# The statistics of the last layer: most of their combining moved into the recurrence's last block, on GpSimd

## The chip, the cores and the metric

One core of a Trainium2 chip (trn2) runs one program. The metric is device microseconds for one execution, as the median of several runs. The engines are TensorE (PE in the profile; its weight loads are PEld), VectorE (DVE), ScalarE (ACT), GpSimd (POOL) and SyncE (SP), which here only issues transfers. The engines run side by side, each its own list of instructions in order, and wait for each other through semaphores.

## What is computed

The reference takes x of shape (8, 32, 256, 256), in fp32, through four layers. Each adds its result to its input, and each normalises its input first (group norm, 16 groups of two channels):

```python
x = x + L0(gn(x))   # Fourier layer: 32 x 32 low modes, mixed over channels
x = x + L1(gn(x))   # one 5 x 5 convolution for every channel
x = x + L2(gn(x))   # recurrence over the 256 columns: a gated cell, 3 rows wide
x = x + L3(gn(x))   # running maxima in four directions, mixed over channels
def _gn(v, G=16, eps=1e-5):
    g = v.reshape(B_, G, C_ // G, H_, W_)
    m = jnp.mean(g, axis=(2, 3, 4), keepdims=True)
    s = jnp.var(g, axis=(2, 3, 4), keepdims=True)
    return ((g - m) / jnp.sqrt(s + eps)).reshape(v.shape)
```

The change concerns the mean and the variance that the last of these normalisations needs: one pair for each image and each pair of channels, over all of the output of the third layer.

## The kernel before

The kernel has three stages, one after the other: the Fourier layer with the convolution (to about 952 us), the recurrence with the running maxima towards the right (to about 2314 us), and the other maxima with the last mixing.

**Recurrence** (`recurrence`, L787). The 256 columns are cut into 32 blocks of 8 (`NB`, `WB`). A column is done in two half steps, x = 0 and x = 1, with four images each; below, half steps are counted n = 2 * column + x within a block, so those with x = 0 are even and those with x = 1 odd. In a half step (`step`, L916) TensorE forms the gates' sums, ScalarE their sigmoids (L937, L939, L940) and the tanh (L944), VectorE the four elementwise steps L938, L943, L951 and L953, whose result is the new state hs. GpSimd does two: the product L946 (one gate times the normalised column xn), for which L951 is made to wait, and the sum L954, which adds the new state to the layer's input and so makes the layer's output in place, in the block's tile xw. Between L946 and L954 the program can put one more instruction for GpSimd: in block 0 it is a normalisation (L838), in half steps 2 to 5 and 8 to 11. All other normalisations are ScalarE's (L842).

Finished blocks leave work for the steps that follow, one piece in each half step, in front of L951: in even ones the running maximum fm of a column (L975), in odd ones the statistics of one image of the block before (L986, a bn_stats instruction that gives counts, means and sums of squared deviations for two halves of its 512 elements). So the statistics of block 30 are made during block 31, and those of block 31, eight instructions, after the last step. SP stores the blocks to memory (L964): x3d, the layer's output, and fwd, the running maxima.

**Combining.** The tile bst holds for every partition, image and block two triples (count, mean, sum of squared deviations); `parts` shows it as 64 triples for each image, so means lie three elements apart. L1020 to L1024 square all the means, add the sums of squared deviations over the count, sum both over the 64 halves, and divide by 64. The matrix `pair` (1/8 where two channels are of one group) then adds up partitions of a group in one matmul (L1075).

**Maxima** (`maxima_and_mix`, L1027) go through the blocks from the last to the first. Blocks 30 and 31 come first: x3_30, x3_31 and fw_30 are loaded through ScalarE's queue (L1117, L1123) in that order, behind all that ScalarE has to do for the recurrence, fw_31 through SP's. The order of VectorE's work is written out by hand: the first maximum of block 30 (L1153), the four short steps of the variance (L1078 to L1081) with a power on GpSimd (L1082) behind them, further maxima (L1156, L1163), the scaled weights (L1087 to L1094), and so on; L1146 is the first instruction that reads x3_31, and L1148 makes the running maximum towards the left, rv.

**Memory.** Pools of tiles are laid one above the other. The recurrence's small pool (`bc`: states, bst, second) lies under its pools for xn, xw, fm and the working tiles. The third stage lays its own pools over the same memory, so its first loads wait for the last readers of the tiles beneath.

Of the kernel before, what the change touches and what calls it, by code (L numbers as in the profile page):

```python
# [9 lines left out]
F32 = mybir.dt.float32  # L10
AF = mybir.ActivationFunctionType
ALU = mybir.AluOpType
AX = mybir.AxisListType
# [3 lines left out]
P = 128  # L17
B, C, H, W = 8, 32, 256, 256
# [6 lines left out]
Q = H // A  # L25
# [761 lines left out]
def recurrence(tc, k, d, x2d, x3d, fwd, stb, first, loaded, mean1, mv3):  # L787
# [4 lines left out]
    nc = tc.nc  # L792
    WB = 8
    NB = W // WB
    NH = 4
    NC = 2
    BC = B // NC
    with ExitStack() as ctx:
        one = ctx.enter_context(tc.tile_pool(name="bc", bufs=1, reuse_waits="tile"))
# [19 lines left out]
        for t in hs[0] + hs[1]:  # L819
            nc.vector.memset(t[:, :, 0 : Q + 2 : Q + 1], 0.0)  # L820
        bst = one.tile([P, B, NB, 6], F32, name="bst")

        raws, norms, psums = {}, {}, {}

# [29 lines left out]
        def free(ins):  # L854

            if some[0]:
                tc.declare_no_dep(ins.ins, group="signals", reason="later matmuls of the same half step end last")
# [28 lines left out]
        def own(n, gate):  # L886

            w, x = divmod(n, NC)
            if w >= W:
                return  # L890
            key = ("r", "z", "nh")[gate]
            out = psums[n, key] = ps.tile([P, BC, Q], F32, name=f"{key}_{n}", tag=f"{key}{x}")
            within(out, OWN, gate, norms[w // WB][:, x * BC : (x + 1) * BC, w % WB, :], True, gate == N)
# [22 lines left out]
        def step(w, x, extra=None):  # L916
            bi, wi = w // WB, w % WB
            bs = slice(x * BC, (x + 1) * BC)
            raw, cur = raws[bi][:, bs, wi, :], norms[bi][:, bs, wi, :]
            new = hs[x][w % NH][:, :, 1 : 1 + Q]  # L920
            if w == 0:
                nc.vector.tensor_copy(new, cur)
            else:
                n, prev = NC * w + x, hs[x][(w - 1) % NH]
                if n == NC:
                    for gate in (Z, R, N):
                        own(n, gate)
                    nc.tensor.drain().then_inc(sem, 1)
                    count[0] += 1
                gates(n, prev)  # L930
                p = {g: psums.pop((n, g)) for g in ("r", "z", "ni", "nh")}
                r = wk.tile([P, BC, Q], F32, name=f"rs_{w}_{x}", tag=f"rs{x}")
                m = wk.tile([P, BC, Q], F32, name=f"n_{w}_{x}", tag=f"n{x}")
                zm = wk.tile([P, BC, Q], F32, name=f"zm_{w}_{x}", tag=f"zm{x}")
                a = wk.tile([P, BC, Q], F32, name=f"a_{w}_{x}", tag=f"a{x}")
                z = wk.tile([P, BC, Q], F32, name=f"zs_{w}_{x}", tag=f"zs{x}")
                rs = nc.scalar.activation(r, p["r"], AF.Sigmoid, bias=brz[:, 0:1])  # L937
                nc.vector.scalar_tensor_tensor(m, p["nh"], bhh[:, 2:3], r, ALU.add, ALU.mult)  # L938
                zms = nc.scalar.activation(zm, p["z"], AF.Sigmoid, bias=brz[:, 2:3], scale=-1.0)  # L939
                zs = nc.scalar.activation(z, p["z"], AF.Sigmoid, bias=brz[:, 1:2])  # L940
                for reader in (rs, zms, zs):
                    free(reader)
                nc.vector.tensor_tensor(m, p["ni"], m, ALU.add)  # L943
                nc.scalar.activation(m, m, AF.Tanh, bias=bih[:, 2:3])  # L944

                product = nc.gpsimd.tensor_tensor(a, zm, cur, ALU.mult)  # L946
                if extra:
                    normalise(*extra, True)
                if pieces[x]:
                    pieces[x].pop(0)()  # L950
                ins = nc.vector.tensor_tensor(m, m, z, ALU.mult)  # L951
                tc.add_manual_dep(ins.ins, product.ins.name, AFTER, reason="the sum behind it then need not wait")
                free(nc.vector.tensor_tensor(new, m, a, ALU.add))  # L953
            nc.gpsimd.tensor_tensor(raw, raw, new, ALU.add)  # L954
# [26 lines left out]
        def finish(bi):  # L981
            raw = raws[bi]
            store(bi, x3d, raw, 6 if bi == NB - 1 else 0)
            for b in range(B):
                pieces[1].append(
                    lambda b=b: nc.vector.bn_stats(bst[:, b, bi, :], raw[:, b].rearrange("p w q -> p (w q)"))  # L986
                )

        with tc.manual_schedule(engines=None):
            load(0)  # L990
            load(1)
            for b in range(B):
                normalise(0, b, 0)
            for b in range(BC):
                normalise(0, b, 1, True)
            other = {2 + b: (0, BC + b, 1) for b in range(BC)}
            other.update({8 + b: (1, b, 0) for b in range(BC)})
            for bi in range(NB):
                for wi in range(WB):
                    if wi == WB // 2 and bi + 2 < NB:  # L1000
                        load(bi + 2)
                    for x in range(NC):
                        n = NC * wi + x
                        step(bi * WB + wi, x, None if bi else other.get(n))
                        if bi + 1 < NB and (bi or wi > 1):
                            half, b = divmod(n, B)
                            normalise(bi + 1, b, half)
                    running(bi, wi)
                    if bi == NB - 1 and wi in (3, 5):
                        store(bi, x3d, raws[bi], wi - 3 if wi == 3 else 4, wi + 1)  # L1010
                finish(bi)
            tc.declare_fence(nc.tensor.drain().ins, group="signals")
            for piece in pieces[0] + pieces[1]:
                piece()

        with tc.manual_schedule(engines=None):
            parts = bst.rearrange("p b n (h k) -> p b (n h) k", k=3)
            n = 2 * NB
            second = one.tile([P, B, n], F32, name="second")
            nc.vector.tensor_tensor(second, parts[:, :, :, 1], parts[:, :, :, 1], ALU.mult)  # L1020
            nc.vector.scalar_tensor_tensor(second, parts[:, :, :, 2], n / float(W * Q), second, ALU.mult, ALU.add)
            nc.vector.tensor_reduce(mv3[:, :, 0], parts[:, :, :, 1], AX.X, ALU.add)
            nc.vector.tensor_reduce(mv3[:, :, 1], second, AX.X, ALU.add)
            nc.vector.tensor_scalar_mul(mv3, mv3, 1.0 / n)  # L1024


def maxima_and_mix(tc, k, d, x3d, fwd, mv3, mean1, out):  # L1027
# [6 lines left out]
    with ExitStack() as ctx:  # L1034
# [206 lines left out]
        with tc.manual_schedule(engines=None):  # L1241
            load_x(NB - 2, nc.scalar)
            load_x(NB - 1, nc.scalar)
            load_f(NB - 2, nc.scalar)
            load_f(NB - 1, nc.sync)
            constants()
            sums()
            order("m10")
# [59 lines left out]
def constants():  # L1308

    n = np.arange(256)  # L1310
    ky = np.arange(KM)
    f = np.concatenate([np.arange(KM), np.arange(-KM, 0)])

    def angle(f, t):
        return 2.0 * np.pi * (np.outer(f, t) % 256) / 256.0

    a = angle(n, ky)
    fw = np.stack([np.cos(a), -np.sin(a)], 1).reshape(2, P, 2, KM).transpose(1, 0, 2, 3)
    a = angle(n, f)
    co, si = np.cos(a), np.sin(a)  # L1320
    co, si = co.reshape(256, 2, 1, KM), si.reshape(256, 2, 1, KM)
    fh = np.stack([np.concatenate([co, -si], 2), np.concatenate([si, co], 2)], 1)
    fh = np.tile(fh.reshape(8, 32, 2, P).transpose(1, 2, 0, 3), (4, 1, 1, 1))
    sign = np.where(np.arange(P) % 64 < 32, 1.0, -1.0)[:, None]

    i = np.arange(P)
    sel = (i[:, None] < C) * (i[:, None] // 2 == np.arange(NG)) / (2.0 * H * W)
    msel = (i[:, None] < C) * (i[:, None] // 2 == i % C // 2) / (2.0 * H * W)
    wc = TS * np.array(BLOCKS)[:, None] + np.arange(32)[None, :]
    c = np.where(ky == 0, 1.0, 2.0)[:, None] / (H * W)  # L1330
    g = angle(ky, wc.reshape(-1))
    gw = np.concatenate([np.cos(g) * c, -np.sin(g) * c] * 2, 0).reshape(2, 2, 2, KM // 2, NT * 32)
    gw = gw.transpose(0, 2, 1, 3, 4).reshape(P, NT, 32)
    e = angle(f, n.reshape(Q, A).T.reshape(-1))
    eh = np.concatenate([np.cos(e), -np.sin(e)], 0)
    ident = np.eye(P)
    ident32 = np.tile(np.eye(C), (4, 1))


    i = np.arange(P) % 32  # L1340
    valid = np.stack([i >= 0, i < 28, i >= 2, i < 30, (i >= 2) & (i < 30)], 1) / (2.0 * H * W)
    valid = np.repeat(valid[:, :, None], P, 2)
    i = np.array(ORDER * A) // 2
    pair = (i[:, None] == i[None, :]) / 8.0
    both = {"fh": fh, "fw": fw, "sign": sign, "sel": sel, "msel": msel, "gw": gw, "eh": eh, "ident": ident, "ident32": ident32, "pair": pair, "valid": valid}
    return {name: np.ascontiguousarray(v, dtype=np.float32) for name, v in both.items()}

# [77 lines left out]
```

## Time and profile before

| | |
|---|---|
| median of 3 runs | 2963.0 us (2962.78, 2963.0, 2967.18) |
| the profiled execution | 2964.42 us, of which the span 2962.6 us |
| VectorE busy in the span | 2572.3 us (87%), 5128 instructions |
| TensorE busy | 2768.3 us (93%) |
| ScalarE busy | 1891.5 us (64%) |
| GpSimd busy | 896.3 us (30%), 1272 instructions |
| granted TensorE clock, mean | 0.973 |

The page comes from one execution on the chip. It divides the span into 40 equal slices and gives each engine's busy share in tenths (9 is 90% or more). A timeline lists instructions in order of time: start and duration in us, engine, line of the kernel, operation, output and inputs by the program's names, partitions x elements, and how many; in square brackets it has the idle time of the engine before the instruction and what ended it. SPq and ACTq are the instructions with which these engines issue transfers. "L1020" is line 1020 of the kernel before.

### The profile page before, as it was taken

The numbers are of one execution on the slowest core, as the hardware profiler recorded it, in microseconds if no ns is written. First come the engines' busy times: TensorE is split into PE (matmuls) and PEld (weight loads), VectorE is DVE, ScalarE is ACT, GpSimd is POOL, SyncE is SP. The second block draws the span as 40 slices with busy tenths as digits, with TensorE's granted clock in tenths as the row PEclk, the third lists the DMA queues.
The fourth block names the chain that finished last, engine by engine and source line by source line (L and its number), as shares of the span: only waits on it lengthen the run. The fifth ranks groups of instructions, "written<-read, shape, count | busy, mean of one in ns | idle before, by whom it ended". The sixth has DMA issues, their size and how long they took to land.

```text
span 2962.6 us, 109979 instructions
## 1 busy us (share of the span) xinstructions
PE 2768.3 (93%) x46856; PEld 1639.5 (55%) x46856; DVE 2572.3 (87%) x5128; ACT 1891.5 (64%) x4465; POOL 896.3 (30%) x1272
## 2 busy tenths in 40 slices
PE   8997999999997999999999999999999588888887
PEld 5665444544444666666666666666666233333333
DVE  5754888888886899999999999999999999999998
ACT  4654677766775888888888888888887222222222
POOL 0112122122212655555555555555555200000000
PEclk9999999999998999999999999999999799999999
DMA  9987677777766676667667766776675698888886
GB/s 400 396 315 277 209 231 229 222 234 228 220 212 156 131 169 140 140 156 168 140 138 159 165 141 140 160 162 141 141 162 124 214 373 322 327 324 322 334 330 241
DMA packets 428195, 651.39 MB, mean 220 GB/s; under 512 B 279208, under 2 KB 283192, under 8 KB 403256
## 3 DMA queue, kind: packets, MB, share of 16 engines
q1 hardware_dynamic: 398872, 488.02, 57.7%
q0 software_dynamic: 15328, 77.36, 7.6%
q10 hardware_dynamic: 13504, 78.98, 6.7%
q8 instruction: 367, 6.01, 0.8%
q14 instruction: 124, 1.02, 0.1%
HBM read 371.63 MB, written 272.63 MB: 217 GB/s over the span
## 4 chain that ended last, share of the span: by engine, by line
PE 45%; DVE 19%; issue 2%; DMA 1%; ACT 0%; SPq 0%; POOL 0%; DVEq 0%; ACTq 0%
PE r L862 14%; PE z L862 13%; PE ni L862 7%; PE nh L862 7%; DVE rv L1148 4%; DVE dq L1163 3%; DVE uq L1165 2%; DVE m L1168 2%; DVE m L1174 2%; DVE m L1171 2%; PE o L1180 2%; DVE top L1156 1%; PE r L870 1%; PE z L870 1%; PE ni L870 1%
## 5 line engine op out<-in xcount | busy, mean ns | idle before, releaser
L870 PE MATMUL z<-hs,weights 64*64 64x256 f32 x4080 | 539.1, 382 | 0.0
L954 POOL TENSOR_TENSOR xw<-xw,hs 128x256 f32<-128x256 f32 x496 | 340.4, 686 | 632.1 <-DVE hs L953 629.0
L870 PE MATMUL r<-hs,weights 64*64 64x256 f32 x4080 | 524.9, 375 | 0.0
L870 PE MATMUL ni<-hs,weights 64*64 64x256 f32 x4080 | 524.9, 375 | 0.0
L1230 ACT ACTIVATE ot<-o,bres 128x512 f32<-128x512 f32 x248 | 150.2, 688 | 478.0 <-PE o L1180 463.2
L608 DVE SCALAR_TENSOR_TENSOR x<-vp,r,x 128x128 f32<-128x128 f32 (+2 forms) x640 | 350.6, 563 | 96.1 <-PE vp L575 84.1
L575 PE MATMUL vp<-x,c_conv 64*64 64x384 f32 (+5 forms) x4608 | 422.4, 491 | 0.4 <-DVE x L608 0.4
L944 ACT ACTIVATE n<-n,bih 128x256 f32<-128x256 f32 x510 | 259.4, 509 | 182.9 <-DVE n L943 182.9
L946 POOL TENSOR_TENSOR a<-zm,xn 128x256 f32<-128x256 f32 x510 | 373.3, 732 | 3.6 <-ACT zm L939 3.5
L862 PE MATMUL r<-hs,weights 64*64 64x256 f32 x2040 | 319.0, 389 | 1.1
L862 PE MATMUL z<-xn,weights 64*64 64x256 f32 x2040 | 305.3, 376 | 11.1 <-ACT xn L842 11.1
L575 PEld LDWEIGHTS vp<-x,c_conv 64*64 64x64 f32 x4608 | 222.0, 132 | 167.8 <-issue 88.8
L1180 PE MATMUL o<-m,wsc 32*32 32x512 f32 x3072 | 220.6, 700 | 93.8 <-DVE m L1174 93.8
L862 PE MATMUL nh<-xn,weights 64*64 64x256 f32 x2040 | 305.7, 376 | 0.0
L862 PE MATMUL r<-xn,weights 64*64 64x256 f32 x2040 | 305.3, 376 | 0.0
L862 PE MATMUL z<-hs,weights 64*64 64x256 f32 x2040 | 305.2, 376 | 0.0
L862 PE MATMUL ni<-hs,weights 64*64 64x256 f32 x2040 | 304.9, 375 | 0.0
L842 ACT ACTIVATE xn<-xw,shift,turned 128x256 f32<-128x256 f32 x492 | 288.4, 586 | 0.0
L870 PEld LDWEIGHTS ni<-hs,weights 64*64 64x64 f32 x4080 | 284.5, 133 | 0.3
L938 DVE SCALAR_TENSOR_TENSOR n<-nh,bhh,rs 128x256 f32<-128x256 f32 x510 | 246.3, 483 | 43.2 <-ACT rs L937 28.7
L870 PEld LDWEIGHTS r<-hs,weights 64*64 64x64 f32 x4080 | 280.9, 131 | 0.2
L937 ACT ACTIVATE rs<-r,brz 128x256 f32<-128x256 f32 x510 | 241.7, 474 | 58.1 <-PE r L870 37.6
(180 smaller groups left out, 6259.2 us busy)
## 6 DMA issues: line engine op xcount, KB each, us to landing
xb<-in_xl_dram POOLq DMA_DIRECT2D x90, 768.0 KB, 7.4
xa<-in_xt_dram SPq DMA_DIRECT2D x64, 1024.0 KB
fwd<-fm SPq DMA_DIRECT2D x256, 256.0 KB
xw<-x2d SPq DMA_DIRECT2D x248, 256.0 KB
fw<-fwd SPq DMA_DIRECT2D x31, 2048.0 KB
out_dram<-ot ACTq DMA_DIRECT2D x62, 1024.0 KB
x3d<-xw SPq DMA_DIRECT2D x240, 256.0 KB
x<-x3d SPq DMA_DIRECT2D x30, 2048.0 KB
```

The lines of the kernel that those rows point to most:

```text
L575: ins = nc.tensor.matmul(vps[bank][to, :, dst], lhsT=k.conv[r, P : P + 64] if kind == 2 else k.conv[r, o], rhs=pair_of(u, ch, g, lo, hi, s ...
L608: nc.vector.scalar_tensor_tensor(x, src[o], r1[rows, g : g + 1], x, ALU.mult, ALU.add, accum_out=s1[rows, 0, n, ch, g : g + 1])
L842: nc.scalar.activation(norms[bi][:, b, w], raws[bi][:, b, w], AF.Identity, bias=shift[:, b : b + 1], scale=sc[:, 1, b : b + 1])
L862: ins = nc.tensor.matmul(out[r], lhsT=weights[r, kind, gate, :], rhs=src[r], start=start, stop=stop)
L870: ins = nc.tensor.matmul(out[pairs[1 - i]], lhsT=weights[r, kind, gate, :], rhs=prev[r, :, q0 : q0 + Q], start=False, stop=stop,)
L937: rs = nc.scalar.activation(r, p["r"], AF.Sigmoid, bias=brz[:, 0:1])
L938: nc.vector.scalar_tensor_tensor(m, p["nh"], bhh[:, 2:3], r, ALU.add, ALU.mult)
L944: nc.scalar.activation(m, m, AF.Tanh, bias=bih[:, 2:3])
L946: product = nc.gpsimd.tensor_tensor(a, zm, cur, ALU.mult)
L954: nc.gpsimd.tensor_tensor(raw, raw, new, ALU.add)
L1180: nc.tensor.matmul(banks[bi][b2][i][32 * j : 32 * j + 32].rearrange("p (w q) -> p w q", q=Q), lhsT=wsc[q, b2, t, :], rhs=src[j][q, b2], st ...
L1230: nc.scalar.activation(ot[:, i], banks[bi][b2][i], AF.Identity, bias=bres[:, b2, i : i + 1])
```

## The change

In each of the first ten half steps of block 31, one GpSimd instruction is put between L946 and L954. The ten of them combine the statistics of blocks 0 to 29 (60 of the 64 halves): square and scale for each group of four images, add, and fold twice, until 15 sums of second moments and 15 sums of means are left for each image, in the tile `sums`. In the last block's own tail VectorE does the same for blocks 30 and 31 (four halves), puts their values beside the 15, and one reduction sums the 19. The division by 64 goes into the matrix `pair`. Four small tiles (`means`, `second`, `scaled`, `sums`) take 5,056 bytes of a partition where `second` took 2,048.

```diff
         bst = one.tile([P, B, NB, 6], F32, name="bst")
+        parts = bst.rearrange("p b n (h k) -> p b (n h) k", k=3)
+        most, count2 = 2 * (NB - 2), W * Q / (2 * NB)
+        means = one.tile([P, B, most // 2], F32, name="means")
+        second = one.tile([P, B, most], F32, name="second")
+        scaled = one.tile([P, BC, most], F32, name="scaled")
+        sums = one.tile([P, 2, B, most // 4 + 4], F32, name="sums")
...
                 product = nc.gpsimd.tensor_tensor(a, zm, cur, ALU.mult)
-                if extra:
+                if callable(extra):
+                    extra()
+                elif extra:
                     normalise(*extra, True)
...
+        def early():
+            gp, h, q = nc.gpsimd, most // 2, most // 4
+
+            def of(x):
+                bs = slice(x * BC, (x + 1) * BC)
+                return [
+                    lambda: gp.tensor_tensor(second[:, bs], parts[:, bs, 0:most, 1], parts[:, bs, 0:most, 1], ALU.mult),
+                    lambda: gp.tensor_scalar_mul(scaled, parts[:, bs, 0:most, 2], 1.0 / count2),
+                    lambda: gp.tensor_tensor(second[:, bs], second[:, bs], scaled, ALU.add),
+                ]
+
+            return of(0) + of(1) + [
+                lambda: gp.tensor_tensor(second[:, :, 0:h], second[:, :, 0:h], second[:, :, h:most], ALU.add),
+                lambda: gp.tensor_tensor(sums[:, 1, :, 0:q], second[:, :, 0:q], second[:, :, q:h], ALU.add),
+                lambda: gp.tensor_tensor(means, parts[:, :, 0:h, 1], parts[:, :, h:most, 1], ALU.add),
+                lambda: gp.tensor_tensor(sums[:, 0, :, 0:q], means[:, :, 0:q], means[:, :, q:h], ALU.add),
+            ]
...
                         n = NC * wi + x
-                        step(bi * WB + wi, x, None if bi else other.get(n))
+                        if bi == NB - 1:
+                            other = dict(enumerate(early()))
+                        step(bi * WB + wi, x, other.get(n) if bi in (0, NB - 1) else None)
...
-            parts = bst.rearrange("p b n (h k) -> p b (n h) k", k=3)
-            n = 2 * NB
-            second = one.tile([P, B, n], F32, name="second")
-            nc.vector.tensor_tensor(second, parts[:, :, :, 1], parts[:, :, :, 1], ALU.mult)
-            nc.vector.scalar_tensor_tensor(second, parts[:, :, :, 2], n / float(W * Q), second, ALU.mult, ALU.add)
-            nc.vector.tensor_reduce(mv3[:, :, 0], parts[:, :, :, 1], AX.X, ALU.add)
-            nc.vector.tensor_reduce(mv3[:, :, 1], second, AX.X, ALU.add)
-            nc.vector.tensor_scalar_mul(mv3, mv3, 1.0 / n)
+            last = parts[:, :, most:]
+            nc.vector.tensor_tensor(sums[:, 1, :, most // 4 :], last[:, :, :, 1], last[:, :, :, 1], ALU.mult)
+            nc.vector.scalar_tensor_tensor(
+                sums[:, 1, :, most // 4 :], last[:, :, :, 2], 1.0 / count2, sums[:, 1, :, most // 4 :], ALU.mult, ALU.add
+            )
+            nc.vector.tensor_copy(sums[:, 0, :, most // 4 :], last[:, :, :, 1])
+            nc.vector.tensor_reduce(mv3.rearrange("p b k -> p k b"), sums, AX.X, ALU.add)
...
-    pair = (i[:, None] == i[None, :]) / 8.0
+    pair = (i[:, None] == i[None, :]) / (8.0 * 64)
```

## The prediction

> **What bounds the kernel now.** I read the page's busy shares by slice first, then the timeline of VectorE across the hand-over from the recurrence to the maxima, then the DMA queues there, and last GpSimd and VectorE in the one stretch where GpSimd already does extra work inside the recurrence. A slice is 74 us; the recurrence ends in slice 32, the maxima fill the rest.
>
> ```profile
> DVE  5754888888886899999999999999999999999998
> ...
> POOL 0112122122212655555555555555555200000000
> ```
>
> From slice 33 on VectorE is never idle: each of the 30 blocks of maxima takes 19.4 us of it (L1153 starts at 2388.46, then at 2407.84). So whatever moves VectorE's first instruction of that stage moves the end by as much. In the recurrence GpSimd is half busy. Its idle half is what the change wants to use. The hand-over, VectorE's timeline:
>
> ```profile
> 2312.98 0.42 DVE L953 TENSOR_TENSOR hs<-n,a 128x256 f32<-128x256 f32 x1
> 2314.19 0.69 DVE L975 TENSOR_TENSOR fm<-xw,fm 128x512 f32<-128x512 f32 x1 [0.79 <-POOL xw L954]
> 2314.80 4.84 DVE L986 BATCH_NORM_STATS2 bst<-xw 128x6 f32<-128x512 f32 x8
> 2319.67 0.83 DVE L1020 TENSOR_TENSOR second<-bst 128x512 f32<-128x512 f32 x1
> 2320.54 0.84 DVE L1021 SCALAR_TENSOR_TENSOR second<-bst,second 128x512 f32<-128x512 f32 x1
> 2321.29 0.82 DVE L1022 TENSOR_REDUCE mv<-bst 128x8 f32<-128x512 f32 x1
> 2322.02 0.68 DVE L1023 TENSOR_REDUCE mv<-second 128x8 f32<-128x512 f32 x1
> 2322.74 0.18 DVE L1024 TENSOR_SCALAR mv<-mv 128x16 f32<-128x16 f32 x1
> 2322.83 2.35 DVE L1153 TENSOR_TENSOR x<-x 128x2048 f32<-128x2048 f32 x1
> ```
>
> The five instructions L1020 to L1024 stand between the last statistics and L1153 with no gap: 2322.83 - 2319.67 = 3.16 us, all on the path. The DMA queues beside them:
>
> ```profile
> 2312.20 10.76 ACTq L1117 DMA_DIRECT2D x<-x3d  x2
> ...
> 2320.51 13.86 SPq L964 DMA_DIRECT2D fwd<-fm x8
> ```
>
> The first of the two loads from ScalarE's queue, x3_30 at 2312.20, is what L1153 reads. When did it land? In the program the first store of fm waits for it, and its other wait, L975, was over at 2314.88; it issued at 2320.51. So x3_30 was there at about 2320.5, 2.3 us before L1153: nearly the next wait already.
>
> **What the change takes away at the hand-over.** Four smaller instructions replace the five. A 128x32 one on VectorE took 0.19 (L1091), and dependent small ones start 0.20 apart (L1079 at 2325.30, L1080 at 2325.50). So 0.20 + 0.20 for square and multiply-add, 0.15 for the copy, which waits for nothing. The reduction of 304 elements to 16 lies between L1024 (0.18, 16 elements) and L1023 (0.68, 512); by elements, 0.15 + 0.53 x 304/512 = 0.46. Sum 1.0; VectorE would be ready at 2320.7 instead of 2322.83. Ends for the four: 0.7 and 1.6, so 2.5 to 1.6 us saved.
>
> Then the load. The tiles added to the recurrence's pool lift everything above them by 3,008 bytes, and x3_30 now overlaps the end of xn_31: in the program its load gains a wait for GpSimd's last product, L946, which ran 2311.67 to 2312.39. It issued at 2312.20, so it moves some 0.3 us, landing near 2320.8. L1153 then starts there: **2.0 us saved**, with 1.2 (load later by 0.8 more) and 2.3 (load not later) as ends. What else moves there costs nothing: the matmul of the statistics (0.58) and the steps behind it hide under L1153's 2.35; the power on GpSimd (L1082, 2.60) hides under L1156 and L1163 (3.6 together), and GpSimd is free for it at 2323.0, 0.9 before it would be asked. Without that cover it costs its 2.60 once. The division goes into a matrix that is loaded anyway. The load of x3_31 loses its wait for the last statistics, but at 2322.63, when it issued, these had long ended (2319.64): the last stores of x3d held it, and still do. It landed near 2334.07 (the last fm store waits for it) and is wanted by L1146 at 2336.46 - 2.0 = 2334.5: 0.4 left, so no cost taken, at most a few tenths. The load of x3_29 follows VectorE's own L1148 and moves with it.
>
> **What the change adds in the recurrence.** Ten GpSimd instructions, one in each of the first ten half steps of block 31, between the product L946 and the sum L954. None issues a DMA. Behind each stand L954, and behind that the next product, which VectorE's L951 waits for. Idle there:
>
> ```profile
> 2295.77 0.73 POOL L946 TENSOR_TENSOR a<-zm,xn 128x256 f32<-128x256 f32 x1
> 2297.66 0.69 POOL L954 TENSOR_TENSOR xw<-xw,hs 128x256 f32<-128x256 f32 x1 [1.15 <-DVE hs L953]
> 2298.30 0.73 POOL L946 TENSOR_TENSOR a<-zm,xn 128x256 f32<-128x256 f32 x1
> 2300.45 0.69 POOL L954 TENSOR_TENSOR xw<-xw,hs 128x256 f32<-128x256 f32 x1 [1.42 <-DVE hs L953]
> ```
>
> 1.15 and 1.42 us are free in turn, so by room alone an instruction of 0.7 us is hidden. Block 0 says otherwise: there the normalisation L838 stands in the same place in eight half steps. Two odd half steps, with it and without:
>
> ```profile
> 970.28 0.56 POOL L838 TENSOR_SCALAR xn<-first,turned,shift 128x256 f32<-128x256 f32 x1
> ```
>
> ```profile
> 970.41 0.70 DVE L951 TENSOR_TENSOR n<-n,zs 128x256 f32<-128x256 f32 x1 [0.65 <-ACT n L944]
> ...
> 975.95 0.43 DVE L951 TENSOR_TENSOR n<-n,zs 128x256 f32<-128x256 f32 x1 [0.64 <-ACT n L944]
> ```
>
> L951 takes 0.70 instead of 0.43 and ends 0.27 after GpSimd's instruction does: VectorE is held by it. By the starts of L953 in even half steps (962.63, 968.25, 973.95, 979.20, 984.70, 990.39, 995.64), a column took 5.62, 5.70, 5.50, 5.69 where an odd half step had L838 and 5.25, 5.25 where none had; 22.51 - 4 x 5.26 = 1.47 us, 0.37 for an odd one. L838 in an even half step shows no cost (5.25 with one).
>
> Five odd ones at 0.37 make 1.8. The new instructions are not L838: by L1069 (32 elements, 0.25) and L946/L954 (256, 0.71) a two-input one has 0.19 + 2.05 ns an element, so 0.68 for 240 (six of them), 0.43 for 120 (two), 0.53 for the two multiplies by L838's rate. In odd half steps that is 0.05 less in all than L838's 0.56 five times; in even ones four are 0.12 longer, of which I take half, 0.24. Five of the ten read every third element. GpSimd shows no such read; on VectorE L1022 (every third) took 0.14 more than L1023 for 512, so 0.07 each, 0.3 in all. **Lost: 1.8 - 0.05 + 0.24 + 0.3 = 2.3 us.** Ends: nothing, if the loop absorbs them (a gain is excluded: nothing is taken out of these columns); and 4.0, if 240 elements go at L443's 2.71 ns each (0.84 with the fixed 0.19; eight at 0.28 over L838 are 2.2 more).
>
> Two rules speak against the change. "SBUF — State Buffer", section "SBUF: two separate sides", says that VectorE with two SBUF inputs and GpSimd share a port pair which one instruction holds to its end. If L951 then ran its full 0.43 after GpSimd's end, each odd half step would lose 0.16 more than by the rows above, 0.8 in all; the row (0.27 after) decides. "GPSIMD Engine Reference", section "Performance pitfalls for Q7 kernels", puts reads with steps over 8 bytes at some 50% more per element; here the step is 12 bytes. As an estimate that makes 0.25 on three two-input instructions and 0.17 on two multiplies, 1.1 us in place of my 0.3; no row here shows it.
>
> **The sum.** 2.3 lost - 2.0 saved = +0.3 us. The profiled execution took 2964.42 (span 2962.6), so 2964.7 for its like; against the median of the three runs, 2963.0, it is **2963.3**. What a measurement of this kernel can tell from no change is about 0.2%, 5.9 us; my forecast is inside it.
>
> **Rivals.**
> - Hidden extras: GpSimd's idle 1.15 and 1.42 us take all ten. For it: room. Against: L951 at 0.70 in block 0. Then -2.0: 2961.0, still no change by the bound. Chance 0.15.
> - The wait takes the removed work's place further: x3_30 lands later still, since its stores and loads share the queues' time, and the lost columns reach their upper end: 4.0 - 1.2 = +2.8: 2965.8. For it: 0.3 us of slack or less at both loads. Chance 0.2.
> - Slower: GpSimd's instructions have a long fixed time when their kind changes. L208 took 1.17 for one element behind a power, L1067 0.76 for 32 where L1069 took 0.25. With 1.17 + 0.49 each is 1.66, 1.1 over L838; ten times 1.1 on top of 1.8 lose 12.8, less 2.0: +10.8, 2973.8. It decides from an average of 1.17 us each (1.8 + 10 x 0.61 - 2.0 = 5.9). Against: L838 kept to 0.56 between L946 and L954. Chance 0.1.
> - Faster by over 5.9 us has no row: all of the removed work is 3.16 us. Only placement that I do not see could do it. Chance 0.05.
>
> The forecast has the other 0.5. Same: 0.5 + 0.15 + 0.2 = 0.85; slower 0.10; faster 0.05. The range takes in -2.3 (nothing lost, 2.3 saved) and +2.8, and about as much as medians of so few runs move (2962.78 to 2967.18 here): 2960.5 to 2967.0.
>
> **What would show it.** Right: L1153 starts at once behind x3_30's load, about 2 us nearer to the last L953 than the 9.85 us here (2322.83 - 2312.98); block 31's first five columns take 5.5 to 5.8 us, with odd L951 at 0.7 to 0.85, and the later ones 5.26; blocks of maxima stay at 19.4. Wrong: columns at 5.26 (rival one), ten instructions well over 1.2 us (rival three), a gap in front of L1146, or a change anywhere before block 31.

## The result and the profile after

The changed kernel takes 2968.8 us (median of 22; 2965.0 to 2971.0) against 2964.3 (median of 22; 2961.6 to 2968.5) for the kernel before on the same chips. The ratio is 1.0013 with a 95% interval of 1.0007 to 1.0019: 3.9 us more, 2.1 to 5.6. (The medians lie 4.5 apart, the means 3.7.) That is inside the 0.2% which was called no change, but it is a real loss where +0.3 was forecast, and the time is 1.8 above the end of the range. About 1 us of that is the yardstick: the first three runs of the kernel before had a median of 2963.0, 22 have 2964.3.

The new lines run some 8 to 27 higher: the state is now L961 (was L953), the sum that waits for GpSimd L959 (L951), the first maximum L1180 (L1153), the copies that need the power L1114 (L1087), the power L1109 (L1082), the sums of weights on GpSimd L1094 to L1098 (L1067 to L1071). The ten new instructions are L1003 to L1005, twice, and L1009 to L1012.

The page of the kernel after, the busy tenths by slice:

```profile
DVE  6754888888886899999999999999999899999998
...
POOL 0112122222212555555555555555556200000000
```

The GpSimd slice in which block 31 lies went from 5 to 6; other digits changed by one where no code did. Slices of 74 us are too coarse for 4, so the reading goes by marks on VectorE. Block 31 is the time from the last state of block 30 to its own last one: 42.52 us before, **45.69 after**. (In the 42.52 one half step is 3.09 long where its like take 2.80; the tail-only kernels below, with the same block 31, have 42.2 to 42.3.) From the last state to the first maximum: 9.85, then 8.87. From there to the copies that need the power 6.48, then 8.11. From the last state to L1146 (now L1173), the first use of x3_31: 23.49, then **24.15**. From the third first-maximum to the last one: 562.65 in both. So the loss is 3.2 in block 31 and 0.66 in the hand-over, 3.8 together, as large as the 3.7 to 4.5 of the whole times. The 2.0 to be saved are not there. The last state of block 30, the first use of x3_31 and the first maximum of block 31 in VectorE's timeline, kernel before, then kernel after:

```profile
2270.46 0.42 DVE L953 TENSOR_TENSOR hs<-n,a 128x256 f32<-128x256 f32 x1
...
2336.46 0.42 DVE L1146 COPY rv<-x 128x512 f32<-128x512 f32 x1
...
2344.59 2.28 DVE L1153 TENSOR_TENSOR x<-x 128x2048 f32<-128x2048 f32 x1
```

```profile
2268.61 0.43 DVE L961 TENSOR_TENSOR hs<-n,a 128x256 f32<-128x256 f32 x1
...
2338.45 0.42 DVE L1173 COPY rv<-x 128x512 f32<-128x512 f32 x1
...
2346.57 2.28 DVE L1180 TENSOR_TENSOR x<-x 128x2048 f32<-128x2048 f32 x1
```

The hand-over in the timeline of VectorE, kernel after (start, duration, engine, line):

```profile
2314.30 0.43 DVE L961 TENSOR_TENSOR hs<-n,a 128x256 f32<-128x256 f32 x1
...
2321.00 0.20 DVE L1046 TENSOR_TENSOR sums<-bst 128x32 f32<-128x32 f32 x1
2321.23 0.20 DVE L1047 SCALAR_TENSOR_TENSOR sums<-bst,sums 128x32 f32<-128x32 f32 x1
2321.34 0.17 DVE L1050 COPY sums<-bst 128x32 f32<-128x32 f32 x1
2321.55 0.47 DVE L1051 TENSOR_REDUCE mv<-sums 128x16 f32<-128x304 f32 x1
2323.16 2.29 DVE L1180 TENSOR_TENSOR x<-x 128x2048 f32<-128x2048 f32 x1 [1.14 <-DMA x<-x3d]
...
2331.27 0.69 DVE L1114 COPY st<-st_c 32x4 f32<-32x4 f32 x4 [1.52 <-POOL st_c L1109]
```

The short tail took 1.0 us (2321.00 to 2322.02). VectorE then stood 1.14 for the load of x3_30 and, new, 1.52 for GpSimd's power. The chain of waits of the same kernel says what held the power (start, duration, what; backwards from the end, here in order of time):

```profile
2314.80 0.62 POOL xw L962
2315.43 7.08 DMA w<-in_w3T_dram
...
2322.58 0.26 POOL wsum L1094
...
2323.24 2.34 POOL wsum L1096
...
2325.96 1.43 POOL wsum L1098 x2
...
2327.54 3.71 POOL st_c L1109
2331.27 0.16 DVE st L1114
```

The path no longer runs through VectorE. It runs through the load of the weights w and then through GpSimd: sums over 32 elements, one of which took 2.34 us, and a power of 3.71. The 2.34 end 0.13 after L1180, which VectorE runs from 2323.16 to 2325.45. In the kernel before, GpSimd's timeline has the same instructions earlier against VectorE's: the first beside the two-input L1021, the others beside one-input reductions (L1022, L1023), the last of them over 0.20 after the first maximum, which needs two inputs, begins:

```profile
2320.70 0.76 POOL L1067 TENSOR_TENSOR wsum<-w 128x32 f32<-128x32 f32 x1 [2.39 <-DMA w<-in_w3T_dram]
2321.55 0.91 POOL L1069 TENSOR_TENSOR wsum<-wsum,w 128x32 f32<-128x32 f32 x3
2322.52 0.51 POOL L1071 COPY wsum<-wsum 128x32 f32<-128x32 f32 x3
2325.96 2.60 POOL L1082 TENSOR_TENSOR st_c<-ve_c,c_mhalf 128x8 f32<-128x8 f32 x1 [2.92 <-DVE ve_c L1081]
```

Inside block 31, GpSimd and VectorE of the kernel after, an even half step (the first line of each) and the next odd one:

```profile
2276.35 1.15 POOL L1005 TENSOR_TENSOR second<-second,scaled 128x240 f32<-128x240 f32 x1
...
2279.66 0.60 POOL L1003 TENSOR_TENSOR second<-bst 128x240 f32<-128x240 f32 x1
```

```profile
2275.91 1.03 DVE L983 TENSOR_TENSOR fm<-xw,fm 128x512 f32<-128x512 f32 x1
2276.86 0.92 DVE L959 TENSOR_TENSOR n<-n,zs 128x256 f32<-128x256 f32 x1
...
2279.80 0.73 DVE L959 TENSOR_TENSOR n<-n,zs 128x256 f32<-128x256 f32 x1
```

L959 takes 0.42 when GpSimd is idle. Here it ends 0.28 and 0.27 after GpSimd's instruction (2277.78 after 2277.50; 2280.53 after 2280.26). And in the even half step GpSimd itself takes longer: L1005 took 1.15 there, beside the running maximum L983, which has two inputs too, and 0.69 in an odd half step, beside one-input statistics. It ended 0.56 after L983 did.

### The profile page after: what moved, and what is told of

It reads as the page before. It is cut to its first block, busy times and chain, and to the rows that moved or that the text cites. A ratio compares the mean times of both kernels' runs of the same rounds, so it can differ in the third digit from the quotient of the medians.

```text
span 2966.7 us, 109988 instructions
## 1 busy us (share of the span) xinstructions
PE 2772.1 (93%) x46856; PEld 1637.5 (55%) x46856; DVE 2574.3 (87%) x5127; ACT 1891.1 (64%) x4465; POOL 909.5 (31%) x1282
## 4 chain that ended last, share of the span: by engine, by line
PE 71%; DVE 21%; DMA 3%; issue 3%; ACT 1%; POOL 1%; SPq 0%; ACTq 0%; DVEq 0%; POOLq 0%
PE r L868 14%; PE vp L575 13%; PE z L868 13%; PE ni L868 7%; PE nh L868 6%; PE up L504 4%; DVE rv L1175 4%; PE yp L143 3%; DVE dq L1190 2%; DVE uq L1192 2%; DVE m L1195 2%; DVE m L1201 2%; DVE m L1198 2%; PE tp L487 2%; PE sp L170 2%
```

## The experiments

Two theories were set against each other. **A**: in the recurrence the ten cost because they read while VectorE runs instructions with two inputs, and at the hand-over the gain is lost in the wait for the power, behind the sums of weights. **B**: the loss comes from elsewhere: GpSimd merely being occupied between product and sum, or the shifted addresses and the later load. "Last state", "first maximum" and "copies" are the marks used above, whatever their line.

**The ten alone, the old tail.** All four new tiles lie in a pool above, so that nothing else moves; `early()` and its call are those of the change, and the five instructions of the old tail stay.

```diff
+        above = ctx.enter_context(tc.tile_pool(name="bt", bufs=1, reuse_waits="tile"))
+        means = above.tile([P, B, most // 2], F32, name="means")
...
```

> The kernel before with the ten GpSimd instructions of the change alone: their tiles lie above all others, so that every other tile keeps its address, nobody reads their result, and the tail on VectorE is the old one. Block 31 (last L953 of block 30 to last L953 of block 31) takes 42.5 us in the kernel before and 45.7 in the changed one. Theory A (GpSimd's instructions hold VectorE's two-input steps): block 31 takes 45.7, the way from the last L953 to the first maximum L1153 stays at 9.85, and the whole is 3.2 us slower. Theory B (the shift of the tiles in memory makes the loss): block 31 stays at 42.5 and the whole within 0.5 us.

Measured 2968.5 against 2965.0, ratio 1.0012 (1.0003 to 1.0021). Block 31 is 45.65, all half steps as in the kernel after; from the last state on all is as before (9.90, 16.38, 23.53). The ten by themselves lose in block 31 what the whole change loses there, and addresses have no part in that. By the whole times the two can't be told apart.

**The tail alone**, without the ten, with the addresses kept (first kernel) and, by a pad of 960 elements, shifted as in the change (second). The tail and `pair` are those of the change; there is no `early()`, so the sums of blocks 0 to 29 are left out of the statistics (zero).

```diff
+        sums = one.tile([P, 2, B, most // 4 + 4], F32, name="sums")
+        one.tile([P, 208], F32, name="pad")
+        nc.vector.memset(sums, 0.0)
...
```

> The kernel before with the short tail alone, four VectorE instructions for blocks 30 and 31; the sums over blocks 0 to 29 are left out (zero), so the statistics are not those of the whole. Every tile keeps its address. Theory A (the power on GpSimd loses its cover: GpSimd's sums of weights now meet L1153 on VectorE): L1153 starts 7.5 to 7.8 us after the last L953 in place of 9.85, but L1087, which needs the power, starts 15.5 to 16.3 after it in place of 16.33, and the whole gains 0 to 0.8 us. Theory B (the loss at the hand-over comes from the shift in memory alone): L1087 starts at 14.1 and the whole gains 2.1.

> The short tail alone as in e2 (sums over blocks 0 to 29 left out), with 3,008 bytes more under the tiles above, as in the changed kernel, so that the load of x3_30 waits for the last product. Theory A: x3_30 lands 0.3 us later than in e2, L1153 starts at 7.8 to 8.1, the rest as in e2. Theory B (the shift costs what the changed kernel shows): L1153 at 8.9 and L1087 at 17.0 after the last L953, 1 us or more slower than e2.

Measured 1.0004 (0.9995 to 1.0012) and 1.0002 (0.9993 to 1.0012): no gain. Block 31 is 42.27 and 42.28. The first maximum came at 7.66, 2.2 earlier than before, with the addresses kept; the copies at 16.26, 0.08 earlier. VectorE and GpSimd of the first kernel:

```profile
2322.47 2.29 DVE L1157 TENSOR_TENSOR x<-x 128x2048 f32<-128x2048 f32 x1
...
2331.07 0.69 DVE L1091 COPY st<-st_c 32x4 f32<-32x4 f32 x4 [2.00 <-POOL st_c L1086]
```

```profile
2322.70 2.18 POOL L1071 TENSOR_TENSOR wsum<-w 128x32 f32<-128x32 f32 x1 [2.55 <-DMA w<-in_w3T_dram]
2324.96 1.84 POOL L1073 TENSOR_TENSOR wsum<-wsum,w 128x32 f32<-128x32 f32 x3
2326.86 2.52 POOL L1075 COPY wsum<-wsum 128x32 f32<-128x32 f32 x3
2329.36 1.69 POOL L1086 TENSOR_TENSOR st_c<-ve_c,c_mhalf 128x8 f32<-128x8 f32 x1
```

The first sum of weights, 0.25 us when nothing is beside it, begins 0.23 after the maximum and ends 0.12 after it. The last input of the power is ready at 2325.56; the power begins at 2329.36. Whatever the tail saves goes into the wait of 2.00. The shifted addresses cost 0.33 more (copies at 16.59, L1146's counterpart at 23.77 instead of 23.44).

**The change, with the power ahead of the sums of weights.** One move on GpSimd, of this line and the two loops behind it: the sums are needed only after the copies.

```diff
-            nc.gpsimd.tensor_tensor(wsum[:, 0], w3[:, 0], w3[:, 1], ALU.add)
...
             nc.gpsimd.tensor_tensor(q4[:, :, 1], ve, k.mhalf[:, :B], ALU.pow)
+            nc.gpsimd.tensor_tensor(wsum[:, 0], w3[:, 0], w3[:, 1], ALU.add)
...
```

> The changed kernel with GpSimd's sums of weights (L1094 to L1098) put behind the power L1109 in its order, nothing else. Theory A (the power was late because these sums stood in front of it, slowed by L1180 on VectorE): L1114 starts 15.3 to 15.6 us after the last L961 in place of 16.97, and the whole is 1.4 us faster than the changed kernel, 2 to 3 slower than the kernel before. Theory B (the power itself is slowed): L1114 stays at 16.5 or later and nothing is gained.

Measured 1.0009 (1.0000 to 1.0018). The copies are at 14.88 (the kernel after: 16.97), better than the expected 15.3 to 15.6. GpSimd, then VectorE:

```profile
2328.20 2.59 POOL L1104 TENSOR_TENSOR st_c<-ve_c,c_mhalf 128x8 f32<-128x8 f32 x1 [6.18 <-DVE ve_c L1103]
2330.77 0.91 POOL L1105 TENSOR_TENSOR wsum<-w 128x32 f32<-128x32 f32 x1
```

```profile
2329.27 2.36 DVE L1190 TENSOR_TENSOR_SCAN dq<-cuts,top 128x1056 f32<-128x1056 f32 x1
2331.55 0.67 DVE L1114 COPY st<-st_c 32x4 f32<-32x4 f32 x4
```

No idle time stands ahead of L1114, and the use of x3_31 comes at 22.12: 2.03 earlier than in the kernel after, 0.41 of it because x3_30 landed earlier in this execution, and 1.37 earlier than before. So of the 2.0 that were forecast for the hand-over 1.4 were there to be had in this kernel; the order on GpSimd took them. The same move is made once more below, on another kernel. It also frees the power of the wait for w, which stands ahead of the sums. That wait alone does not explain the delay: in the kernel after, w had landed by 2322.58, and with the 0.25, 0.91 and 0.51 that they take in the kernel with the ten alone the sums would have been over by about 2324.4, an estimate from these rows; the power's last input was ready at 2326.19.

**The change with old addresses** (`means`, `second` and `scaled` in the pool above, a filler below).

```diff
+        means = above.tile([P, B, most // 2], F32, name="means")
+        one.tile([P, 208], F32, name="pad")
```

> The changed kernel with its new tiles above all others (sums and a filler where second was), so that every other tile keeps the address it has in the kernel before. From the last L953 of block 30 to the first maximum of block 29 it is 98.1 us in the kernel before and 102.5 in the changed one. Theory A (GpSimd and VectorE hold each other up, the addresses cost 0.3): 102.0 to 102.3, with block 31 at 45.7. Theory B (the addresses cost most of it): 98 to 99.5.

Measured 1.0007 (0.9998 to 1.0016): block 31 45.63, first maximum 7.64, copies 16.23, use of x3_31 23.41. The mark of block 29 came at 101.26, 0.7 under the expectation. That mark holds a load that varies from 23.1 to 24.8 between kernels of like work, so the later tables use the first maximum of block 31 instead. Theory A holds for block 31. At the use of x3_31 the same code is 0.74 better with old addresses, in one execution of each; the landing of x3_30 varies by as much (7.5 to 8.4 among kernels with old addresses). So the 0.66 that the change loses in the hand-over seem to come with the addresses or the loads; the 2.0 are absent either way.

**Ten instructions that only write.** Are the ten dear because GpSimd is occupied? The kernel before, with a memset of 720 elements in each place.

```diff
+                            other = {i: lambda: nc.gpsimd.memset(blank, 0.0) for i in range(10)}
```

> The kernel before with ten memsets of 128x720 on GpSimd (0.67 us each by the rate of L1065, 1056 elements in 0.98) in the ten places, to a tile that nobody reads; the tail is the old one. They read nothing. Theory A (GpSimd's reads hold VectorE's two-input steps): block 31 stays at 42.5 (up to 42.8). Theory B (ten more instructions in GpSimd's order delay the sum and the product behind them, whatever they do): block 31 takes 44.5 or more.

Measured 0.9996 (0.9987 to 1.0005). GpSimd's timeline, then VectorE's, an even half step:

```profile
2270.34 0.73 POOL L948 TENSOR_TENSOR a<-zm,xn 128x256 f32<-128x256 f32 x1
2271.01 0.70 POOL L1009 MEMSET blank<- 128x720 f32 x1
2272.49 0.69 POOL L958 TENSOR_TENSOR xw<-xw,hs 128x256 f32<-128x256 f32 x1 [0.79 <-DVE hs L957]
```

```profile
2270.67 0.94 DVE L979 TENSOR_TENSOR fm<-xw,fm 128x512 f32<-128x512 f32 x1
2271.54 0.41 DVE L955 TENSOR_TENSOR n<-n,zs 128x256 f32<-128x256 f32 x1
```

0.70 us each, in the very place and as long as the adds, and block 31 is 42.53, the 42.52 of the kernel before (with the same long half step in it): nothing lost, L955 at 0.41. Occupation is free; B falls for the recurrence. The Trainium skill's "SBUF — State Buffer", section "Who interferes with whom", says that a VectorE instruction with two SBUF inputs contends with a GpSimd instruction that reads SBUF and not with one that only writes; this run agrees.

**By input count and half step.** Three kernels put contiguous instructions of 240 elements in block 31: ten with one input; five with two inputs in the even half steps; five in the odd ones. Of each edit only the new instruction and its half steps are printed:

```diff
+ gp.tensor_scalar_mul(blank[:, 2], blank[:, 0], 1.0)                      for i in range(10)
+ gp.tensor_tensor(blank[:, 2], blank[:, 0], blank[:, 1], ALU.add)         for i in range(0, 10, 2)
+ gp.tensor_tensor(blank[:, 2], blank[:, 0], blank[:, 1], ALU.add)         for i in range(1, 10, 2)
```

> The kernel before with ten GpSimd multiplies by a constant (one input, 240 elements side by side, tiles above all others, nobody reads the result) in the ten places. Theory A (the prediction's price from block 0 holds for instructions of L838's kind, one input: 0.37 us in an odd half step, nothing in an even one; the changed kernel lost more because most of its ten have two inputs): block 31 takes 44.0 to 44.5. Theory B (block 0's even half steps hid a cost that any reading instruction has in block 31): 45 or more, with even half steps at 3.1 instead of 2.8.

> The kernel before with five GpSimd additions (two inputs, 240 elements side by side, nobody reads the result) in half steps 0, 2, 4, 6 and 8 alone. Theory A (two-input instructions hold L951 behind the running maximum): 0.4 to 0.5 us each, block 31 at 44.5 to 45.0. Theory B (the even half steps are free as the prediction had it, the cost is in the odd ones): 42.5 to 42.9.

> The same five additions in half steps 1, 3, 5, 7 and 9 alone. Theory A: 0.2 to 0.35 us each, block 31 at 43.5 to 44.2, less than in the even ones. Theory B: 45 or more, all of the changed kernel's loss.

| | block 31 | lost | each, even / odd | ratio |
|---|---|---|---|---|
| ten with one input | 43.51 | 1.31 | 0.19 / 0.06 | 1.0006 (0.9997 to 1.0015) |
| five with two, even | 44.65 | 2.45 | 0.50 / none | 1.0006 (0.9997 to 1.0016) |
| five with two, odd | 44.06 | 1.86 | none / 0.36 | 1.0010 (1.0001 to 1.0019) |

The loss is against 42.2, and each is the mean growth of one half step, against the 2.79 of an even and the 2.49 of an odd one in the first tail-only kernel. The 0.36 is a hair over its expectation of 0.2 to 0.35. The five even ones are the clearest. GpSimd, then VectorE:

```profile
2273.74 1.14 POOL L1010 TENSOR_TENSOR blank<-blank 128x240 f32<-128x240 f32 x1
```

```profile
2273.38 0.95 DVE L980 TENSOR_TENSOR fm<-xw,fm 128x512 f32<-128x512 f32 x1
2274.25 0.91 DVE L956 TENSOR_TENSOR n<-n,zs 128x256 f32<-128x256 f32 x1
```

The running maximum ends at 2274.33, GpSimd's add 0.55 later, L956 0.28 after that: two waits one behind the other. The one-input kernel in an even half step, GpSimd and then VectorE:

```profile
2272.72 1.25 POOL L1010 TENSOR_SCALAR blank<-blank 128x240 f32<-128x240 f32 x1
```

```profile
2273.22 0.60 DVE L956 TENSOR_TENSOR n<-n,zs 128x256 f32<-128x256 f32 x1
```

It is longer than the add (1.25), and yet L956 ends before it does (2273.82 against 2273.97). That one missed its expectation: 44.0 to 44.5 was expected, from 0.37 an odd half step as in block 0. VectorE does not come later here: in block 0 L951 began 0.13 after L838 (970.41 after 970.28) and took 0.70, in block 31 L956 began 0.14 after the multiply (2275.85 after 2275.71) and took 0.52. Block 0 has both outcomes itself: its L951 at 981.36, 0.13 after another L838, took 0.43. Why a one-input instruction sometimes lets VectorE go sooner than a two-input one is open.

**On ScalarE instead.** The same combining, three instructions for each image that sum as they go, two in each half step n = 0 to 11 of block 31; the second kernel, run twice, has the power first as well. Printed are the three instructions alone, without the loop over the images:

```diff
+ nc.scalar.activation(rest, means, Square, accum_out=sums[:, 1, b, 0:1])
+ nc.scalar.activation(rest, means, Identity, accum_out=sums[:, 0, b, 0:1])
+ nc.scalar.activation(rest, m2, Identity, scale=1.0 / count2, accum_out=sums[:, 1, b, 1:2])
```

> Blocks 0 to 29 combined by ScalarE instead of GpSimd: 24 activations of 60 elements with a running sum each (square of the means, means, sums of squared deviations), two in each of the first twelve half steps of block 31; the short tail on VectorE; addresses as in the kernel before. Theory A (the port of GpSimd and VectorE is the cost in block 31, the power's lost cover the one behind it): block 31 at 42.5, the power late as in the short tail alone, first maximum of block 29 at 97.8 to 98.3 us, no change in the whole. Theory B (any engine's extra work in block 31 costs, since the loop has no room): block 31 at 44 or more, and slower by that.

> As e7_scalar, with GpSimd's sums of weights behind its power. Theory A: L1087 14.0 to 14.4 us after the last L953 (16.33 before), first maximum of block 29 at 95.7 to 96.1 us (98.1 before), 2.0 to 2.4 us faster than the kernel before as a whole. Theory B (another wait takes the place: the load of x3_31 or the matmul of the biases): 97 us or more and 1 us or less gained.

> e8_scalar_power_first once more, to see on other runs whether its 2.1 us show in the time of the whole. Theory A: block 31 at 42.2 and L1087 14.0 to 14.5 after the last L953, ratio to the kernel before 0.9992 to 0.9996. Theory B (what the hand-over gains is lost elsewhere): 1.000 or more.

Measured 0.9996 (0.9987 to 1.0005), 0.9996 (0.9987 to 1.0005) and 0.9997 (0.9988 to 1.0006). Block 31 is 42.19, 42.22 and 42.24: the work costs nothing there. With the old order on GpSimd the copies stay at 16.14, as with the tail alone; with the power first they come at 14.40 and 14.37. So the order is worth 1.7 here, though x3_30 landed 0.4 later in these two. VectorE of the second kernel:

```profile
2318.91 0.25 DVE L1042 TENSOR_REDUCE mv<-sums 128x16 f32<-128x96 f32 x1
2319.64 2.29 DVE L1171 TENSOR_TENSOR x<-x 128x2048 f32<-128x2048 f32 x1 [0.48 <-DMA x<-x3d]
...
2326.06 0.67 DVE L1105 COPY st<-st_c 32x4 f32<-32x4 f32 x4
```

From the last state of block 30 to the first maximum of block 31, a mark that has both parts in it, these are the kernels: before 74.13, after 77.97, the ten alone 77.30, the change with the power first 75.92, ScalarE with the power first **71.99 and 71.98**. By this mark the last is 2.1 better than before and 6.0 better than the change. In the whole time the two runs together have a mean of 2963.5 against 2964.8, 1.3 less; but the memsets, which change neither of these marks, also came out 1.5 less in the mean of theirs. So it is ahead of the change, and whether it beats the kernel before is not shown by the whole times: the 2.0 to 2.4 us that were expected are not in them, nor is a ratio of 0.9996 or less in the second run. The marks of block 29 missed too (96.70 for 97.8 to 98.3; 96.46 for 95.7 to 96.1); they hold the load that varies.

## Why the prediction was wrong

Between the forecast +0.3 and the 3.8 by the marks lie 3.5 us: 2.7 of them in the hand-over, 0.9 in the recurrence.

**The term that failed first: even half steps of the recurrence.** The prediction took 0.24 for all five, since "L838 in an even half step shows no cost". They cost 2.4: 0.41, 0.51, 0.31, 0.41 and 0.73 by the lengths from state to state. L838 has one input, and eight of the ten have two; the prediction did not weigh that here, nor that the running maximum beside them has two as well. The even adds by themselves (0.50 each) show the price of two inputs, the one-input kernel (0.19) that of one.

Nor was L838 free. The prediction measured from start to start of L953, and in an even half step of block 0 it is L953 itself that is late. GpSimd, then VectorE, kernel before, half step 8 of block 0:

```profile
978.27 1.24 POOL L838 TENSOR_SCALAR xn<-xw,turned,shift 128x256 f32<-128x256 f32 x1
```

```profile
979.20 0.59 DVE L953 TENSOR_TENSOR hs<-n,a 128x256 f32<-128x256 f32 x1
```

L953 takes 0.43 in half step 6, which has no L838; here it ends 0.28 after L838 does. The 0.16 lie behind the mark and were counted to the next half step, an odd one. By the ends of L953 the column with L838 in its even half step alone took 5.41, not 5.25, and the two with it in the odd one alone 5.54: 0.29, not 0.37.

**Odd half steps**: 1.75 forecast, 1.0 measured (0.19, 0.27, 0.36, 0.11, 0.10). The rule read from block 0, that VectorE ends 0.27 after GpSimd, holds for two inputs; the two instructions of 120 elements (0.45 and 0.44) are over early and cost a third. The rule of "SBUF — State Buffer", "SBUF: two separate sides", that one instruction holds the ports to its end, would have L959 end 0.42 after; 0.28 was measured, as the prediction took it.

**Strided reads**: 0.3 forecast, and about 0.3 in all. The controls have the same 240 elements contiguous. One input: the half steps grew by 0.31 and 0.19 where the control's grew by 0.19 and 0.06. Two different inputs, even: 0.73 for 0.50 (L1011 took 1.38, a contiguous L1005 1.15). One strided tensor read twice (L1003): 0.41 and 0.27 for 0.50 and 0.36, less and not more; it took 0.60 where a contiguous add took 0.69. So a price was seen in two of three forms, and the sum was right by a saving in the third that nobody had forecast. The 50% of "GPSIMD Engine Reference", "Performance pitfalls for Q7 kernels", is not in L1003.

Sum of the recurrence: 2.3 forecast, 3.2 to 3.4 measured, inside its ends (0 to 4.0). The first five columns took 5.8 to 6.1 where 5.5 to 5.8 was named as the sign of being right.

**The term that failed second: 2.0 saved at the hand-over**, in the step "the power … hides under L1156 and L1163 …, and GpSimd is free for it at 2323.0, 0.9 before it would be asked". From the last state on it was free after 10.1 before and after 13.2 in the change. The step took the time of GpSimd's queue from the trace as fixed. But the 0.91 and 0.51 of its sums of weights were times beside one-input work on VectorE; the change moves a 2.3 us two-input instruction over them. The power began 1.3 after its last input (0.1 before the change) and took 3.73 instead of 2.60; it delayed the copies by 1.52, and the hand-over lost 0.66 where it was to gain 2.0. The prediction had written what it costs if that cover goes; it gave no chance to it.

**Also in the hand-over**: x3_30's wait for xn_31 came as worked out (issue 0.2 later against the last state), but it landed at 8.9 instead of 7.5, so the first maximum came 0.98 earlier, not 2.0. It landed at 7.5 to 8.4 in kernels with old addresses and 8.1 to 8.9 with shifted ones, so part of that is the spread of a load.

**What held**: the four short instructions (1.0), the later columns of block 31 at 5.26, the blocks of maxima unchanged, nothing to wait for at x3_31, nothing upstream. Of the rivals, "the wait takes the removed work's place" (2965.8) was nearest in size and sign, though another wait did it. The fixed price of new kinds of instruction, which was to make the kernel clearly slower, did not show: contiguous adds took 0.69, as the rate from L1069 and L946 had given. "Hidden extras" is refuted by block 31.

## What to carry to other kernels

Idle time on GpSimd is not free time while VectorE runs instructions with two inputs: ask of each added instruction whether it reads, with how many inputs, and what stands beside it on VectorE; a write, or the same work on ScalarE, cost nothing here. When work is taken off the path, look at every short instruction of other engines that used to run under it, and time it again under what runs there next. And order a queue by who waits: five lines moved behind the power gave back 2 us by the marks in one kernel and 1.7 in another.

## What the runs showed of the hardware that was not expected

A GpSimd add of 32 elements, 0.25 us alone, took 2.09 to 2.34 us beside a VectorE instruction of 2.29, and three copies of 32 elements 0.51 to 2.53. The power took 1.68 to 3.73 us for the same 8 elements, by what VectorE ran at the time.

The clock in the last stretch of a run can move the end. Two windows of 3.40 us near the end, after and before (stretch, its length, busy time and instructions of the engines from PE on, granted clock, DMA share, GB/s):

```profile
2949.80:2953.20 3.40, 3.40 (x69) 1.76 (x57) 3.37 (x2) 0.00 (x0) 0.00 (x0) 0.50 0.00 0
```

```profile
2945.70:2949.10 3.40, 2.55 (x78) 1.41 (x90) 3.33 (x4) 0.00 (x0) 0.00 (x0) 1.00 0.00 0
```

At half the clock TensorE is busy all the time there, and the stretch from the last block's first maximum to the end took 32.9 us instead of 31.4. Three of the fourteen profiles have this step in that place and the longer stretch (the change, its version with old addresses, the odd adds). Five others have half the clock for 3.4 to 6.8 us around the start of the stretch, and it takes 31.4 there. The change with the power first has the same work on TensorE as the change and not the longer stretch, so this is probably of the execution and not of the kernel; each kernel but one has a single profile, which does not show it. 1.5 of the 4.1 us between the two profiled spans are this. (The rest: 3.84 by the mark with both parts in it, 0.58 in the load of x3_29, and 1.85 less, since this execution was that much earlier at the last state of block 30.)
